# Four chained transformer layers on one core: layer 3 scales its probabilities ahead of the value product, with a second query buffer and a revised planner

## The chip, the cores and the metric

The kernel runs on one core of one Trainium2 chip. The metric is the device time of one execution in microseconds (us). Three runs of the kernel before gave 2625.58, 2627.42 and 2633.65 us, a median of 2627.42.

## What is computed

There are 64 batches of 128 tokens with 128 features. A context of 77 tokens per batch is shared by the first three layers. Every layer has 16 heads. Layers 0, 1 and 2 are cross-attention layers with heads of 8 features; layer 3 is self-attention with heads of 64 features, in segments of 64 tokens. Cut to layer 3, the reference is:

```
q, k, v = split(rms_norm(x) @ to_qkv_w)        # 16 heads x 64 features
q, k = rope(q), rope(k)
kf = [k_extra x 16, persistent keys x 16, k]   # k_extra: one row per batch, 16 times
vf = [v_extra x 16, persistent values x 16, v]
scores = q . kf * 64**-0.5, masked: causal and same segment, or extra/persistent
probs = softmax(scores)
x = x + (probs . vf) @ to_out_w
x = x + (silu(g) * a) @ ff_w2 + ff_b2          # a, g from rms_norm(x) @ ff_w1
```

The 16 extra keys are equal, so the kernel holds one of them and gives its exponential the weight NM = 16. Per segment there are then KE = 64 + 1 + 16 = 81 keys.

## The kernel before, in words

**Order of the work.** Nothing is issued while the kernel function runs. Each engine call is recorded by a planner (`Plan`, L56). It holds a model of the cost of each operation (`matmul` for TensorE, `other` for the rest, from L137 on), gives each a start time, and at the end issues all calls in the order of those times (`issue`). So the order on every engine's queue, SyncE's DMA queue among them, comes out of the model, and the chip then follows that fixed order, with semaphores for the true dependencies. The layers are written as generators ("threads") in two chains: chain 0 holds layers 0 to 2, chain 1 holds layer 3. The main loop proceeds with the thread whose next operands are ready first; `ahead` is the lead in TensorE work of chain 0 over chain 1, in units of WORK = 71 us, less LEAD = 1.4, and moves the choice towards the chain that is behind. `SWITCH` prices a change of TensorE's tile shape.

**Fills.** Where the planner sees TensorE idle for over 0.4 us, `keep_busy` puts in matmuls whose result nobody reads (`first16` by `ident16`, bf16, 512 or 128 columns), until 0.1 us short of the awaited start. They are in TensorE's stream for good, and their line in the profile is that of the matmul that they precede.

**Tiling.** Layers 0 to 2 go by groups of G = 4 batches (16 groups), and layer 3 by batch within a group. Layers 0 to 2 share `attend` (scores at L675/L684, maximum L696, subtraction L697, exponential L700, transposes of the probabilities by `turned` L635/L636, values L719, division by the sums after the product L739/L741).

**Layer 3, one batch.** `layer3_ahead` computes `rms_scaled` once per group (POOL multiplies four 128x128 blocks at L555) and then, batch by batch, `layer3_projections`: q and k with rotation (`rope`: matmuls L1078, DVE shuffle L1080, POOL L1081 and L1086, DVE L1085) and v (L1108, copied by ACT at L1110/L1111 into `vext` and `vs`; a DMA brings the second segment over). `vext` has 65 columns per head: 64 values and a one, so the value product also gives the sum of the probabilities; the memory row holds 16 times its values and a 16. `layer3_middle` runs `layer3_scores` in two halves of eight heads: a penalty product (L1129: bf16 identity of 128x128 by a mask of 4x81 columns, two per half), then 16 products of 64x64 tiles (L1135), the maximum (DVE L1143) and the subtraction (DVE L1144); one exponential over all 16 heads follows (ACT L1150). `layer3_values` transposes the probabilities (L635/L636) and, in two halves, multiplies them with `vext` (L1171, 81x64 tiles, probabilities stationary, two column tiles), takes the reciprocal of the sum column (L1179), multiplies (DVE L1180) into `o`, transposes `o` with eight 128x128 transposes (L1196, ACT copies L1197) into `oT`, and multiplies with the output weights (L1202, L1204). `layer3_feed_forward` runs once per group. There is one buffer each of `q3`, `o3` and `oT3`. `layer3_ahead` starts the projections of batch i when the scores of i-1 are recorded and the values of i-2.

PSUM has two double banks `sc` (scores, layer 3's values, hidden layers) and four single banks `mm`.

Of the kernel before, what the change touches and what calls it, by code (L numbers as in the profile page):

```python
# [20 lines left out]
P = 128  # L21
# [30 lines left out]

WORK, LEAD = 71.0, 1.4


class Plan:  # L56
# [16 lines left out]
    def __init__(self):  # L73
        self.records = []
        self.lines = {}
        self.past = {}
        self.free = {}
        self.tags = {}
        self.pe, self.shape, self.work = 0.7, (128, 128), 0.0
        self.window, self.use, self.clock = 0.0, 0.0, 1.0  # L80
        self.idle = None
        self.lost, self.switched, self.fills = 0.0, 0.0, 0
        self.block = 0.0, 0.0
# [32 lines left out]

    def after(self, x, write, engine):

        t = 0.0
        p0, p1, f0, f1 = self.reach(x)  # L120
        for q0, q1, g0, g1, own, other, by, wrote in self.past.get(x.name, ()):
            if (write or wrote) and q0 < p1 and p0 < q1 and g0 < f1 and f0 < g1:
                t = max(t, own if by == engine else other + self.SEM)
        return t

    def access(self, x, write, own, other, engine):
# [12 lines left out]
    def matmul(self, dst, w, x, passes, call, line):  # L139
# [15 lines left out]
        else:  # L155
            cost = max(cost * 1.02, 0.05 if half else 0.109)
        cost *= passes
        self.work += cost
        start = max(
            self.pe, self.after(dst, True, "PE"), self.after(w, False, "PE"),  # L160
            self.after(x, False, "PE"),
        )
        if self.idle is not None and start - self.pe > self.FILL:
            self.keep_busy(start - 0.1, shape, line)
        self.run(start, shape, cost, call, line)
        end = self.pe + (0.2 if self.clock == 1.0 else 0.3)
# [3 lines left out]

    def run(self, start, shape, cost, call, line):
        while start - self.window > self.WINDOW:
            share = self.use / self.WINDOW
            self.clock = 0.5 if share < self.SLOW else 1.0 if share > self.FAST else self.clock
            self.use = 0.0
            self.window += self.WINDOW
        switch = self.switch(shape)
        cost /= self.clock
        self.use += switch + cost
        self.lost += cost * (1 - self.clock)  # L180
        self.switched += switch
        self.records.append((start, len(self.records), call, line))
        self.pe = start + switch + cost
        self.shape = shape
# [40 lines left out]
    def other(self, engine, op, args, kw, call, line):  # L225
# [24 lines left out]
        name = engine  # L250
        t = max(0.7, self.pe - self.BEHIND)
        for x in aps:
            t = max(t, self.after(x, any(x is o for o in outs), engine))
        takes = max(cost - hidden, 0.02)
# [76 lines left out]
def four_layers(ctx: ExitStack, tc: tile.TileContext, a: dict, out: bass.AP):  # L331
# [105 lines left out]
    def load_x(g):  # L437
# [6 lines left out]
        {  # L444
            "h": (1, FF * G * P), "o3": (1, 8 * P), "oT3": (1, 8 * P), "q3": (1, 8 * P),
            "vs": (1, 8 * P), "ro": (3, 4 * P),
# [99 lines left out]
    def rms_scaled(x, name):  # L546
# [7 lines left out]
        for b in range(G):  # L554
            pool.tensor_scalar(y[:, b, :], x[:, b, :], r[:, b : b + 1], None, ALU.mult)  # L555
        drop(mv, ms, r)
# [356 lines left out]
    def memory_tokens():  # L913


        mT = const.tile([P, B], F32, tag="mT", name="mT")
        parts = [(att, "s3", H * KE)] * 2 + [(p3, tag, 8 * P) for tag in ("q3", "o3", "oT3")]
        i = 0
# [10 lines left out]
        kmem = const.tile([P, 8, B], F32, tag="kmem", name="kmem")  # L929
        vmem = const.tile([B, H, DH3 + 1], F32, tag="vmem", name="vmem")  # L930
        yield "wait", lambda: 0 in ys or done[0] > 0
# [26 lines left out]
        acte.copy(kmem, pm)  # L958
        dve.memset(vmem[:, :, DH3], float(NM))
        for c in range(2):  # L960
            yield F, tokT, "mm"
            pm = bank([B, 512], f"mem_p4{c}")
            w = wqkv[:, (16 + 4 * c) * P : (20 + 4 * c) * P]
            matmul(pm, tokT, w, start=True, stop=True)

            acte.activation(
                vmem[:, 8 * c : 8 * c + 8, 0:DH3],
                pm.rearrange("p (h d) -> p h d", d=DH3),
                AF.Copy,
                scale=float(NM),  # L970
            )
# [4 lines left out]
    kext = [in_p3.tile([P, 8, 2, KE], F32, tag=f"kext{i}", name=f"kext{i}") for i in range(2)]  # L976
    vext = [in_p3.tile([KE, 2, H, DH3 + 1], F32, tag=f"vext{i}", name=f"vext{i}") for i in range(2)]
    for i in range(2):
        dve.memset(vext[i][:, :, :, DH3], 1.0)
        for s in range(2):  # L980
            sp.dma_start(kext[i][:, :, s, SEG + 1 : KE], a["L3_pmK"])
            sp.dma_start(vext[i][SEG + 1 : KE, s, :, 0:DH3], a["L3_pmV"])
# [135 lines left out]
    def layer3_scores(i, qT):  # L1118
# [4 lines left out]
        for half in range(2):  # L1123
            yield F, qT, kx, "sc"
            pb = two_banks(f"{n}_ps{half}")
            ps = pb[:, :, : 4 * KE].rearrange("p c (j k) -> p c j k", k=KE)
            for c in range(2):
                pen = pen316.unsqueeze(1).to_broadcast([P, 4, KE])
                matmul(ps[:, c], ident16, pen, start=True, stop=False)  # L1129
            for j in range(4):  # L1130
# [11 lines left out]
            m = mx[:, 8 * half : 8 * half + 8].rearrange("p (c j) -> p c j", c=2)  # L1142
            dve.tensor_reduce(m, ps, AX.X, ALU.max)  # L1143
            dve.tensor_tensor(  # L1144
                sc[:, 8 * half : 8 * half + 8, :].rearrange("p (c j) k -> p c j k", c=2),
                ps,
                m.unsqueeze(3).to_broadcast([P, 2, 4, KE]),
                ALU.subtract,
            )
        acte.activation(sc, sc, AF.Exp, scale=DH3**-0.5)  # L1150
        drop(mx, qT)
        return sc

    def layer3_values(i, sc, x):
        n = f"a3_{i}"
        vx = vext[i % 2]
        o = p3.tile([P, 2, 4, 2, DH3], F32, tag="o3", name=f"{n}_o")
        sT = att.tile([KE, H, P], F32, tag="sT3", name=f"{n}_sT")
        for j in range(0, H, 4):
            yield from turned(sT, j, sc.rearrange("p h k -> p (h k)"), KE, n)  # L1160
        drop(sc)
        turned3[0] = i + 1
        for half in range(2):
            yield (128, 64), sT, "sc"
            pb = two_banks(f"{n}_pa{half}")
            pa = pb[:, :, : 4 * (DH3 + 1)].rearrange("p c (j d) -> p c j d", j=4)
            for c in range(2):
                for j in range(4):
                    slot = 4 * (2 * half + c) + j
                    for s in range(2):  # L1170
                        matmul(  # L1171
                            pa[SEG * s : SEG * s + SEG, c, j, :],
                            sT[:, slot, SEG * s : SEG * s + SEG],
                            vx[:, s, head(slot), :],
                            start=True,
                            stop=True,
                        )
            rs = small.tile([P, 2, 4], F32, tag="rsl3", name=f"{n}_rs{half}")
            dve.reciprocal(rs, pa[:, :, :, DH3])  # L1179
            dve.tensor_tensor(  # L1180
                o[:, half].rearrange("p j e d -> p e j d"),
                pa[:, :, :, 0:DH3],
                rs.unsqueeze(3).to_broadcast([P, 2, 4, DH3]),
                ALU.mult,
            )
            drop(rs)
        drop(sT)
        valued3[0] = i + 1
        of = o.rearrange("p a j e d -> p (a j e d)")
        oT = p3.tile([P, 8, P], F32, tag="oT3", name=f"{n}_oT")  # L1190
        for half in range(2):
            yield F, o, "mm"
            pt = bank([P, 4, P], f"{n}_po{half}")
            for j in range(4):
                c = 4 * half + j
                transpose(pt[:, j, :], of[:, c * P : (c + 1) * P])  # L1196
            acte.copy(oT[:, 4 * half : 4 * half + 4, :], pt)  # L1197
        drop(o)
        yield F, oT, "mm"
# [6 lines left out]
    def layer3_feed_forward(g, y):  # L1206
        x = xs[g]
        xT = yield from transposed(y, f"f3_{g}_xT", fnorm, tag="x3")
        drop(y)
        xT = xT.rearrange("p b t -> p (b t)")  # L1210
        u01 = p3.tile([P, 2, G * P], F32, tag="oT3", name=f"f3_{g}_u01")
        u2 = p3.tile([P, 2, G * P], F32, tag="o3", name=f"f3_{g}_u2")
        uT = [u01[:, 0, :], u01[:, 1, :], u2[:, 0, :]]
        for c, (o0, n) in enumerate(FF3):
# [42 lines left out]
    idle = Tiles(  # L1257
        xT=(act, "xT"), kT=(p3, "vs"), v=(p3, "o3"), qT=(p3, "q3"), o=(act, "y3"),
        kb=(p3, "ro"), s=(att, "s3"), sT=(att, "sT3"), w=(act, "x3"),
    )  # L1260

    def early_layer0():
        for g in range(1, 1 + early):
            yield "wait", lambda: fed[0] >= g and begun[0] >= g and plan.free["cT"]
            cT = load_ctx(g)
# [6 lines left out]
    def layers_0_to_2():  # L1272
        yield begun0_at
        o, ready = yield from begun0
        yield "also", layer0_feed_forward(0, o, ready)
        yield "also", early_layer0()
        for g in range(NG):
# [23 lines left out]
    def layer3_ahead():  # L1301
        for i in range(B):
            g, b = divmod(i, G)
            if b == 0:
# [3 lines left out]
                drop(y)  # L1308
            yield "wait", lambda: scored3[0] >= i and valued3[0] >= i - 1
            qs[i] = yield from layer3_projections(i, xT[:, b, :])  # L1310
# [147 lines left out]
```

## Time and profile before

| what | value |
|---|---|
| median of the three runs | 2627.42 us |
| the profiled execution | 2622.82 us |
| its span, first to last instruction | 2621.0 us |
| instructions | 64439 |
| mean granted TensorE clock | 0.983 |
| TensorE (PE) busy | 2473.2 us, 94% |
| VectorE (DVE) busy | 1908.2 us, 73% |
| ScalarE (ACT) busy | 1372.1 us, 52% |
| GpSimd (POOL) busy | 1368.8 us, 52% |
| mean busy share of the DMA engines | about 20% |

"Busy" is the time in which at least one instruction of the engine runs. A float32 matmul stands as two records, and a record runs from its entry to its last result, which is longer than the time after which the next may enter; the rates below are therefore taken from runs of many. A group's row gives line, engine, operation, what is written from what, shapes and count; then busy us and mean ns of one; then the idle time of the engine just before the group, and what ended it. The chain of work is followed back from the last instruction, and its shares tell on which engine and line the time was spent.

### The profile page before, as it was taken

The numbers are of one execution on the slowest core, as the hardware profiler recorded it, in microseconds if no ns is written. First come the engines' busy times: TensorE is split into PE (matmuls) and PEld (weight loads), VectorE is DVE, ScalarE is ACT, GpSimd is POOL, SyncE is SP. The second block draws the span as 40 slices with busy tenths as digits, with TensorE's granted clock in tenths as the row PEclk, the third lists the DMA queues.
The fourth block names the chain that finished last, engine by engine and source line by source line (L and its number), as shares of the span: only waits on it lengthen the run. The fifth ranks groups of instructions, "written<-read, shape, count | busy, mean of one in ns | idle before, by whom it ended". The sixth has DMA issues, their size and how long they took to land.

```text
span 2621.0 us, 64439 instructions
## 1 busy us (share of the span) xinstructions
PE 2473.2 (94%) x26568; PEld 1810.8 (69%) x26568; DVE 1908.2 (73%) x3973; ACT 1372.1 (52%) x2361; POOL 1368.8 (52%) x1421
## 2 busy tenths in 40 slices
PE   7999999999899999999999999999999999999998
PEld 3566776767667776767767777677776667767776
DVE  4656787777877778676876868688775977777664
ACT  2455454556464555546555555545555555554543
POOL 1234646454754655455564645656454654637563
PEclk8999999999999999999999999999999999999999
DMA  5311221212122121211212121211212112121010
GB/s 115 107 26 38 49 41 30 62 27 46 28 47 45 26 66 18 51 34 35 52 20 70 23 49 31 49 39 25 70 17 49 40 32 52 22 58 17 12 19 14
DMA packets 376479, 108.21 MB, mean 41 GB/s; under 512 B 328739, under 2 KB 364920, under 8 KB 376056
## 3 DMA queue, kind: packets, MB, share of 16 engines
q1 hardware_dynamic: 376184, 104.08, 19.4%
q8 instruction: 209, 3.42, 0.5%
q14 instruction: 86, 0.70, 0.1%
HBM read 74.97 MB, written 4.19 MB: 30 GB/s over the span
## 4 chain that ended last, share of the span: by engine, by line
PE 57%; DVE 26%; POOL 6%; issue 5%; ACT 2%; DMA 2%; SPq 1%; DVEq 0%; POOLq 0%; ACTq 0%
PE mm L635 9%; PE mm L1078 5%; PE sc L684 5%; PE mm L567 5%; DVE mx L696 4%; PE sc L825 3%; PE sc L1171 3%; PE mm L719 3%; DVE s L697 3%; DVE s L1003 3%; PE mm L1108 3%; PE mm L1202 3%; DVE s L1001 2%; PE sc L1135 2%; DVE ro L1080 2%
## 5 line engine op out<-in xcount | busy, mean ns | idle before, releaser
L636 ACT COPY sT<-mm 116x512 f32<-116x512 f32 (+2 forms) x832 | 443.3, 585 | 185.6 <-PE mm L635 177.6
L1081 POOL TENSOR_TENSOR ro<-ro,w_c_sin 128x512 f32<-128x512 f32 x256 | 327.6, 1280 | 388.5 <-DVE ro L1080 386.6
L635 PE MATMUL mm<-w_c_ident,s 128*116 128x128 f32 (+2 forms) x3328 | 459.7, 281 | 56.7 <-DVE q L1085 11.2
L700 ACT ACTIVATE s<-s 128x616 f32<-128x616 f32 x384 | 275.4, 717 | 444.2 <-DVE s L697 442.9
L635 PEld LDWEIGHTS mm<-w_c_ident,s 128*116 128x116 f32 (+2 forms) x3328 | 376.2, 145 | 147.9 <-issue 45.5
L520 POOL TENSOR_TENSOR rstd<-rstd,mhalf 128x4 f32<-128x4 f32 x96 | 102.6, 1068 | 401.2 <-DVE rstd L519 384.3
L652 POOL TENSOR_TENSOR kb<-kT,qmask 128x308 f32<-128x308 f32 x184 | 131.8, 726 | 339.7 <-PE sc L684 176.7
L1078 PE MATMUL mm<-x,w_L_to_qkv_w 128*128 128x128 f32 x2048 | 266.2, 279 | 4.1 <-ACT sT L636 2.6
L684 PE MATMUL sc<-kb,qT 32*128 32x308 f32 x1472 | 257.8, 460 | 10.4 <-DVE s L1144 5.5
L696 DVE TENSOR_REDUCE mx<-sc 128x8 f32<-128x616 f32 x256 | 202.8, 792 | 86.4 <-PE sc L684 85.8
L1078 PEld LDWEIGHTS mm<-x,w_L_to_qkv_w 128*128 128x128 f32 x2048 | 243.8, 192 | 24.9 <-issue 12.7
L697 DVE TENSOR_TENSOR s<-sc,mx 128x616 f32<-128x616 f32 x256 | 204.6, 799 | 9.1
L1080 DVE STREAM_SHUFFLE ro<-mm 128x512 f32<-128x512 f32 x256 | 188.3, 735 | 0.6
L719 PE MATMUL mm<-sT,vf 116*32 116x128 f32 (+1 forms) x4608 | 170.7, 278 | 7.0 <-ACT sT L636 4.4
L1086 POOL TENSOR_TENSOR q<-q,ro 128x512 f32<-128x512 f32 x128 | 164.3, 1284 | 10.0
L719 PEld LDWEIGHTS mm<-sT,vf 116*32 116x32 f32 (+1 forms) x4608 | 116.2, 110 | 76.6 <-issue 29.8
L1086 POOL TENSOR_TENSOR kext<-kext,ro 128x512 f32<-128x512 f32 x128 | 155.2, 1212 | 10.0
L1143 DVE TENSOR_REDUCE mx<-sc 128x8 f32<-128x648 f32 x128 | 105.8, 827 | 67.2 <-PE sc L1135 66.3
L1150 ACT ACTIVATE s<-s 128x1296 f32<-128x1296 f32 x64 | 82.2, 1284 | 137.8 <-DVE s L1144 137.6
L684 PEld LDWEIGHTS sc<-kb,qT 32*128 32x128 f32 x1472 | 108.1, 187 | 64.8 <-issue 39.0
L1171 PEld LDWEIGHTS sc<-vext,sT 81*64 81x64 f32 x4096 | 129.2, 139 | 31.0 <-issue 15.4
L1171 PE MATMUL sc<-vext,sT 81*64 81x65 f32 x4096 | 141.6, 226 | 3.8 <-DVE s L697 3.1
(228 smaller groups left out, 4849.1 us busy)
## 6 DMA issues: line engine op xcount, KB each, us to landing
s<-in_fside SPq DMA_DIRECT2D x64, 616.0 KB
vext<-vs SPq DMA_DIRECT2D x64, 256.0 KB
fm<-in_fmask SPq DMA_DIRECT2D x64, 154.0 KB
vf<-v SPq DMA_DIRECT2D x138, 38.5 KB
cT<-in_ctxT SPq DMA_DIRECT2D x32, 154.0 KB
xT<-in_xT SPq DMA_DIRECT2D x16, 256.0 KB
xs<-in_x SPq DMA_DIRECT2D x16, 256.0 KB
out<-y SPq DMA_DIRECT2D x16, 256.0 KB
```

Source lines behind the costliest of these rows:

```text
L635: transpose(pt[:, i, :], s[:, columns(keys, j + i)])
L636: acte.copy(dst[:keys, j : j + 4, :], pt)
L684: matmul(ps[:, c], qT[r, b * P : (b + 1) * P], kb[r], start=pen is None, stop=True,)
L696: dve.tensor_reduce(m, ps, AX.X, ALU.max)
L697: dve.tensor_tensor(d, ps, m.unsqueeze(3).to_broadcast([P, 2, QD, S2]), ALU.subtract)
L700: acte.activation(s[:, h0 : h0 + 8], s[:, h0 : h0 + 8], AF.Exp, scale=scale)
L719: matmul(pa[VC * c : VC * c + VC, x // 2, :], va[:r, x, b, c], sT[:r, j, :], start=x != 1, stop=x != 0,)
L1078: matmul(pq[:, j, :], w, xT, start=True, stop=True)
L1080: dve.stream_shuffle(ro, pq, swap)
L1081: pool.tensor_tensor(ro, ro, sinT.unsqueeze(1).to_broadcast([P, 4, P]), ALU.mult)
L1086: pool.tensor_tensor(d, d, ro, ALU.add)
L1171: matmul(pa[SEG * s : SEG * s + SEG, c, j, :], sT[:, slot, SEG * s : SEG * s + SEG], vx[:, s, head(slot), :], start=True, stop=True,)
```

## The change

- Layer 3 normalises before the value product. The exponential is taken per half; POOL multiplies the memory key's probability by 16, DVE sums, DVE takes the reciprocal, POOL multiplies. `vext` loses its column of ones (65 to 64 columns), and the memory values their factor 16.
- The value product is turned around: `vext` is stationary and the probabilities stream, so that its result is already transposed; the tile `o`, its reciprocal and multiplication, and the eight transposes per batch go. It writes one `mm` bank per half in place of a double bank.
- The penalty product is done in four 64x64 tiles per half.
- `q3` has two buffers, `o3` goes; projections may start one batch earlier. The feed-forward's third block moves from `o3` to `q3`.
- `rms_scaled` multiplies on ACT, not POOL.
- The early layer-0 groups start before the first group's end.
- The planner charges each further semaphore wait of an instruction with 0.05 us (PE, DVE) or 0.017 us, and LEAD is 1.8.

```diff
-WORK, LEAD = 71.0, 1.4
+WORK, LEAD = 71.0, 1.8
...
+    def waits(self, engine, ends):
+        new = [by for by, end in ends.items() if end > self.known.get((engine, by), 0.0)]
+        self.known.update(((engine, by), ends[by]) for by in new)
+        return max(0, len(new) - 1) * (0.05 if engine in ("PE", "DVE") else 0.017)
...
-        self.run(start, shape, cost, call, line)
+        self.run(start, shape, cost, call, line, self.waits("PE", ends))
...
+        cost += self.waits(engine, ends)
...
-            "h": (1, FF * G * P), "o3": (1, 8 * P), "oT3": (1, 8 * P), "q3": (1, 8 * P),
+            "h": (1, FF * G * P), "oT3": (1, 8 * P), "q3": (2, 8 * P),
...
-            pool.tensor_scalar(y[:, b, :], x[:, b, :], r[:, b : b + 1], None, ALU.mult)
+            acte.activation(y[:, b, :], x[:, b, :], AF.Copy, scale=r[:, b : b + 1])
...
-    vext = [in_p3.tile([KE, 2, H, DH3 + 1], F32, tag=f"vext{i}", name=f"vext{i}") for i in range(2)]
+    vext = [in_p3.tile([KE, 2, H, DH3], F32, tag=f"vext{i}", name=f"vext{i}") for i in range(2)]
...
             for c in range(2):
-                pen = pen316.unsqueeze(1).to_broadcast([P, 4, KE])
-                matmul(ps[:, c], ident16, pen, start=True, stop=False)
+                r = slice(SEG * c, SEG * c + SEG)
+                pen = pen316[r].unsqueeze(1).to_broadcast([SEG, 4, KE])
+                for s in range(2):
+                    q = slice(SEG * s, SEG * s + SEG)
+                    matmul(ps[q, c], ident16[r, r], pen, start=True, stop=False)
...
-        acte.activation(sc, sc, AF.Exp, scale=DH3**-0.5)
+            acte.activation(ex, ex, AF.Exp, scale=DH3**-0.5)
+            pool.tensor_scalar(ex[:, :, SEG], ex[:, :, SEG], float(NM), None, ALU.mult)
+            total = small.tile([P, 8], F32, tag="rsl3", name=f"{n}_t{half}")
+            dve.tensor_reduce(total, ex, AX.X, ALU.add)
+            dve.reciprocal(total, total)
+            pool.tensor_tensor(
+                ex, ex, total.unsqueeze(2).to_broadcast([P, 8, KE]), ALU.mult
+            )
...
-            yield (128, 64), sT, "sc"
-            pb = two_banks(f"{n}_pa{half}")
+            yield (128, 64), sT, "mm"
+            pa = bank([P, 4, P], f"{n}_pa{half}")
-            for c in range(2):
-                for j in range(4):
+            for j in range(4):
+                for c in range(2):
                     slot = 4 * (2 * half + c) + j
                     for s in range(2):
                         matmul(
-                            pa[SEG * s : SEG * s + SEG, c, j, :],
+                            pa[DH3 * c : DH3 * c + DH3, j, SEG * s : SEG * s + SEG],
+                            vx[:, s, head(slot), :],
                             sT[:, slot, SEG * s : SEG * s + SEG],
-                            vx[:, s, head(slot), :],
...
-            rs = small.tile([P, 2, 4], F32, tag="rsl3", name=f"{n}_rs{half}")
-            dve.reciprocal(rs, pa[:, :, :, DH3])
-            dve.tensor_tensor(
...
+            acte.copy(oT[:, 4 * half : 4 * half + 4, :], pa)
...
-                transpose(pt[:, j, :], of[:, c * P : (c + 1) * P])
-            acte.copy(oT[:, 4 * half : 4 * half + 4, :], pt)
...
+        yield "wait", free("q3")
-        u2 = p3.tile([P, 2, G * P], F32, tag="o3", name=f"f3_{g}_u2")
+        u2 = p3.tile([P, G * P], F32, tag="q3", name=f"f3_{g}_u2")
...
-            yield "wait", lambda: fed[0] >= g and begun[0] >= g and plan.free["cT"]
+            yield "wait", lambda: fed[0] >= g - 1 and begun[0] >= g - 1 and plan.free["cT"]
...
-            yield "wait", lambda: scored3[0] >= i and valued3[0] >= i - 1
+            yield "wait", lambda: scored3[0] >= i - 1 and valued3[0] >= i - 1 and plan.free["q3"]
```

More of the change, by code (lines that the diff above doesn't have):

```diff
@@ L80, in __init__ @@
         self.window, self.use, self.clock = 0.0, 0.0, 1.0
+        self.known = {}
         self.idle = None
@@ L115, in reach, with after @@
         return p, p + parts, f, f + 1 + sum(abs(s) * (c - 1) for s, c in free)
-    def after(self, x, write, engine):
+    def after(self, x, write, engine, ends=None):
         t = 0.0
@@ L123, in after @@
                 t = max(t, own if by == engine else other + self.SEM)
-        return t
+                if ends is not None and by != engine:
+                    ends[by] = max(ends.get(by, 0.0), other)
+        return t
+    def waits(self, engine, ends):
+        new = [by for by, end in ends.items() if end > self.known.get((engine, by), 0.0)]
+        self.known.update(((engine, by), ends[by]) for by in new)
+        return max(0, len(new) - 1) * (0.05 if engine in ("PE", "DVE") else 0.017)
     def access(self, x, write, own, other, engine):
@@ L158, in matmul @@
         self.work += cost
+        ends = {}
         start = max(
-            self.pe, self.after(dst, True, "PE"), self.after(w, False, "PE"),
-            self.after(x, False, "PE"),
+            self.pe, self.after(dst, True, "PE", ends), self.after(w, False, "PE", ends),
+            self.after(x, False, "PE", ends),
         )
@@ L169, in matmul, with run @@
         self.access(x, False, self.pe, end, "PE")
-    def run(self, start, shape, cost, call, line):
+    def run(self, start, shape, cost, call, line, extra=0.0):
         while start - self.window > self.WINDOW:
@@ L176, in run @@
             self.window += self.WINDOW
-        switch = self.switch(shape)
+        switch = self.switch(shape) + extra
         cost /= self.clock
@@ L251, in other @@
         t = max(0.7, self.pe - self.BEHIND)
+        ends = {}
         for x in aps:
-            t = max(t, self.after(x, any(x is o for o in outs), engine))
+            t = max(t, self.after(x, any(x is o for o in outs), engine, ends))
+        cost += self.waits(engine, ends)
         takes = max(cost - hidden, 0.02)
@@ L916, in memory_tokens @@
         mT = const.tile([P, B], F32, tag="mT", name="mT")
-        parts = [(att, "s3", H * KE)] * 2 + [(p3, tag, 8 * P) for tag in ("q3", "o3", "oT3")]
+        parts = [(att, "s3", H * KE)] * 2 + [(p3, tag, 8 * P) for tag in ("q3", "vs", "oT3")]
         i = 0
@@ L929, in memory_tokens @@
         kmem = const.tile([P, 8, B], F32, tag="kmem", name="kmem")
-        vmem = const.tile([B, H, DH3 + 1], F32, tag="vmem", name="vmem")
+        vmem = const.tile([B, H, DH3], F32, tag="vmem", name="vmem")
         yield "wait", lambda: 0 in ys or done[0] > 0
@@ L958, in memory_tokens @@
         acte.copy(kmem, pm)
-        dve.memset(vmem[:, :, DH3], float(NM))
         for c in range(2):
@@ L964, in memory_tokens @@
             matmul(pm, tokT, w, start=True, stop=True)
[L966 to L970, printed above, removed]
+            acte.copy(
+                vmem[:, 8 * c : 8 * c + 8, :], pm.rearrange("p (h d) -> p h d", d=DH3)
             )
@@ L976, in four_layers @@
     kext = [in_p3.tile([P, 8, 2, KE], F32, tag=f"kext{i}", name=f"kext{i}") for i in range(2)]
-    vext = [in_p3.tile([KE, 2, H, DH3 + 1], F32, tag=f"vext{i}", name=f"vext{i}") for i in range(2)]
+    vext = [in_p3.tile([KE, 2, H, DH3], F32, tag=f"vext{i}", name=f"vext{i}") for i in range(2)]
     for i in range(2):
-        dve.memset(vext[i][:, :, :, DH3], 1.0)
         for s in range(2):
@@ L1123, in layer3_scores @@
         for half in range(2):
-            yield F, qT, kx, "sc"
+            yield (64, 64), qT, kx, "sc"
             pb = two_banks(f"{n}_ps{half}")
@@ L1143, in layer3_scores @@
             dve.tensor_reduce(m, ps, AX.X, ALU.max)
+            ex = sc[:, 8 * half : 8 * half + 8, :]
             dve.tensor_tensor(
-                sc[:, 8 * half : 8 * half + 8, :].rearrange("p (c j) k -> p c j k", c=2),
+                ex.rearrange("p (c j) k -> p c j k", c=2),
                 ps,
@@ L1149, in layer3_scores @@
             )
-        acte.activation(sc, sc, AF.Exp, scale=DH3**-0.5)
+            acte.activation(ex, ex, AF.Exp, scale=DH3**-0.5)
[6 more added lines that the diff above has]
+            )
+            drop(total)
         drop(mx, qT)
@@ L1156, in layer3_values @@
         vx = vext[i % 2]
-        o = p3.tile([P, 2, 4, 2, DH3], F32, tag="o3", name=f"{n}_o")
         sT = att.tile([KE, H, P], F32, tag="sT3", name=f"{n}_sT")
@@ L1162, in layer3_values @@
         turned3[0] = i + 1
+        oT = p3.tile([P, 8, P], F32, tag="oT3", name=f"{n}_oT")
         for half in range(2):
-            yield (128, 64), sT, "sc"
-            pb = two_banks(f"{n}_pa{half}")
-            pa = pb[:, :, : 4 * (DH3 + 1)].rearrange("p c (j d) -> p c j d", j=4)
-            for c in range(2):
-                for j in range(4):
+            yield (128, 64), sT, "mm"
+            pa = bank([P, 4, P], f"{n}_pa{half}")
+            for j in range(4):
+                for c in range(2):
                     slot = 4 * (2 * half + c) + j
@@ L1177, in layer3_values @@
                         )
-            rs = small.tile([P, 2, 4], F32, tag="rsl3", name=f"{n}_rs{half}")
-            dve.reciprocal(rs, pa[:, :, :, DH3])
[L1180 to L1186, printed above, removed]
+            acte.copy(oT[:, 4 * half : 4 * half + 4, :], pa)
         drop(sT)
         valued3[0] = i + 1
[L1189 to L1198, printed above, removed]
         yield F, oT, "mm"
@@ L1210, in layer3_feed_forward @@
         xT = xT.rearrange("p b t -> p (b t)")
+        yield "wait", free("q3")
         u01 = p3.tile([P, 2, G * P], F32, tag="oT3", name=f"f3_{g}_u01")
-        u2 = p3.tile([P, 2, G * P], F32, tag="o3", name=f"f3_{g}_u2")
-        uT = [u01[:, 0, :], u01[:, 1, :], u2[:, 0, :]]
+        u2 = p3.tile([P, G * P], F32, tag="q3", name=f"f3_{g}_u2")
+        uT = [u01[:, 0, :], u01[:, 1, :], u2]
         for c, (o0, n) in enumerate(FF3):
@@ L1257, in four_layers @@
     idle = Tiles(
-        xT=(act, "xT"), kT=(p3, "vs"), v=(p3, "o3"), qT=(p3, "q3"), o=(act, "y3"),
+        xT=(act, "xT"), kT=(p3, "vs"), v=(p3, "oT3"), qT=(p3, "q3"), o=(act, "y3"),
         kb=(p3, "ro"), s=(att, "s3"), sT=(att, "sT3"), w=(act, "x3"),
@@ L1273, in layers_0_to_2 @@
         yield begun0_at
+        yield "also", early_layer0()
         o, ready = yield from begun0
         yield "also", layer0_feed_forward(0, o, ready)
-        yield "also", early_layer0()
         for g in range(NG):
```

## The prediction

> **What bounds the kernel now.** I read the page first: the busy shares, the chain that ended last, then the rows of groups with shapes kept apart, then the time-ordered chain inside one steady stretch.
>
> ```profile
> span 2621.0 us, 64439 instructions
> PE 2473.2 (94%) x26568; PEld 1810.8 (69%) x26568; DVE 1908.2 (73%) x3973; ACT 1372.1 (52%) x2361; POOL 1368.8 (52%) x1421
> PE   7999999999899999999999999999999999999998
> PE 57%; DVE 26%; POOL 6%; issue 5%; ACT 2%; DMA 2%; SPq 1%; DVEq 0%; POOLq 0%; ACTq 0%
> ```
>
> TensorE is busy from the third slice to the end and carries 57% of the chain, VectorE 26%. 2621.0 - 2473.2 = 148 us are without any matmul: by stretches of the trace, 26 us in the first 262, 106 up to 2424, 15 in the last 197. So a matmul taken out pays only if nothing else then holds TensorE up, and VectorE at 73% is the next.
>
> ```profile
> L1171 PE MATMUL sc<-vext,sT 81*64 81x65 f32 x4096 | 141.6, 226 | 3.8 <-DVE s L697 3.1 <-DVE s L1144 0.4
> L1196 PE MATMUL mm<-w_c_ident,o 128*128 128x128 f32 x512 | 74.4, 278 | 3.1 <-DVE o L1180 2.1 <-ACT oT L1197 0.3
> L1129 PE MATMUL sc<-pen,ident 128*128 128x324 bf16 x256 | 56.9, 303 | 4.9 <-DVE s L697 1.8 <-ACT h L827 1.1 <-DVE o L1226 0.6
> L684 PE MATMUL mm<-first,ident 32*128 32x512 bf16 x109 | 26.9, 390 | 0.0
> L1180 DVE TENSOR_TENSOR o<-sc,rsl 128x512 f32<-128x512 f32 x128 | 88.5, 691 | 4.4
> L1081 POOL TENSOR_TENSOR ro<-ro,w_c_sin 128x512 f32<-128x512 f32 x256 | 327.6, 1280 | 388.5 <-DVE ro L1080 386.6 <-ACT s L700 1.7
> L697 DVE TENSOR_TENSOR s<-sc,mx 128x616 f32<-128x616 f32 x256 | 204.6, 799 | 9.1
> L697 DVE TENSOR_TENSOR s<-s,mx 128x616 f32<-128x616 f32 x128 | 120.8, 944 | 4.3
> ```
>
> These are the rows that the change touches or resembles. A matmul's mean holds its latency, so I take rates from runs in the chain in order of time:
>
> ```profile
> 1210.16 0.28 PE sc L1129 x2
> 1210.44 0.77 PE sc L1135 x32
> ...
> 1227.71 1.08 PE sc L1171 x32
> ...
> 1235.72 0.88 PE mm L1196 x8
> ```
>
> **TensorE, what goes.** 512 transposes (L1196) at 0.88/8 = 0.11 us: -56 us (their row's 74.4 holds the tails of 128 sets too, which the next matmul covers). The penalty: two of 0.14 us per half become four in four different 64x64 tiles. If those run side by side, one 0.14 us is left: 128 halves x 0.14 = -17 us. L1135 speaks for it: 32 records of 81 columns in 0.77 us, 24 ns each, against 236 for one. If they ran one after another it would be 0.56 us per half, +35. I take -17. The built programs' TensorE streams have 1139 changes of tile shape after, 1237 before; between the end of the last penalty's 0.14 us (1210.27) and the first L1135 (1210.37) the timeline leaves 0.1 us, so 98 x 0.1 = -10. One column of 65 less: -2. Sum **-85 us**.
>
> **TensorE, what comes.** The built streams hold 608 fills before and 1122 after: 505 to 963 of 512 columns, 103 to 159 of 128. By the row above, 26.9/109 = 0.247 us each (0.14 for the short, L635's 17 took 2.3): 458 x 0.247 + 56 x 0.14 = **+121 us**. By stretches of the stream (first tenth of the real matmuls, middle, last 7.5%) it is 351/160/97 fills before, 311/538/273 after. A fill runs whether or not the wait it covers exists. So TensorE's stream grows by 121 - 85 = +36 us although real work leaves it: the planner sees TensorE waiting longer for others. How much of this falls into idle time is the whole question. The same program with the new charge for waits set to nothing has 910 fills; so 212 of them (50 us) answer to waits that the planner of before did not see, though the chip had them: TensorE's 148 idle us are those. The other 302 (71 us) answer to real waits of the new order. Value taken: the 50 us fall into idle time, so 2621 + 36 - 50 = **2607 us** span. Bounds: none falls there, 2657; or, with the better costs, a third of the 98 us of idle then left goes as well, 2573.
>
> **VectorE.** Out: 128 x 691 (L1180) = -88 us; 128 reciprocals move, 0.2 us each, at nothing. In: 128 sums of 648 columns; the maximum of 616 from SBUF takes 795 ns, so 836 ns: +107. Net +19, 1927 us (74%). It lies beside TensorE in the middle, but all of it is ahead of the values now.
>
> **POOL.** In: 128 products of 648 columns at 1280/512 = 2.5 ns: 1.62 us, +207. 128 multiplications of 8 columns: between the 16-column copy (L1102, 260 ns) and the 128-column L555 (606 ns); taken 0.3, +38. Out: L555, -75. Net +170, 1539 us (59%). Behind each new product on POOL's queue stand rope's L1081/L1086, at 1.28 us each, and layer norms; a rope late by 2 us is hidden while projections run one batch ahead, and costs the 2 us where layer 3 is alone. [...]
>
> **ACT.** The exponential in halves: L700 (616 columns) 717, so 744 ns x 128 - 82 = +13; 128 scalings of 128 columns, L728 at 256 takes 368 ns, taken 0.32: +41. 1426 us (54%), hidden by TensorE. The copies of `oT` stay.
>
> **Latency of a half of layer 3's softmax.** Added: 0.3 + 0.84 + 0.2 + 1.62 = 3.0 us between exponential and transposes; removed behind the values: 0.2 + 0.69 + the transposes' 0.44 and their wait. The second query buffer and scores one batch ahead cover it, with 2621/64 = 41 us per batch. In the last stretch, where layer 3 is alone, the cover is gone; the 176 more fills there (about 40 us) show that, and LEAD 1.8 lengthens this stretch.
>
> **DMA, start.** `vext` rows become contiguous (256-byte pieces become 4 KB); DMA is 2% of the chain, so nothing. On SyncE's queue the early group's x and context move ahead of the second kext load; fills fall from 351 to 311 there, about -10, already in the sum.
>
> **The value product.** Passes now come to one column tile four in a row (two products of two passes), before two and two. No row shows four. L719 has two in a row over four tiles and still keeps them side by side. With side by side kept, 0. If the queue blocked behind a busy tile, eight passes would take 6 slots in place of 4: 64 records in 2.02 us (L1171 in the same chain) are 32 ns each, half more is 4096 x 16 = +65 us. I take 0, by L719.
>
> **The rivals.** (a) As taken: 2607, plus the 1.8 us between span and profiled time, 2609; the median of the runs shown is 4.6 above the profiled one, so 2613. Chance 0.38; own range 2600 to 2630. (b) The new cost model is nearer the chip, waits are filled and ordered better: 2573 span, 2580. For it: three quarters of the idle lies in the middle in small waits. Against: real work in the stream is only 85 us less. Chance 0.22. (c) The other side: fills are too long. The planner charges the 8-column multiplication 1.26 us, where rows say 0.3; TensorE then works through fills for probabilities that are already there, and none of the 121 us falls into idle: 2657 + 6 = 2663. It decides as soon as less than 36 us are covered. Chance 0.25. (d) The column tiles block: 2613 + 65 = 2678; chance 0.09. (e) POOL's longer queue holds up rope in the middle too, 1 us per batch: 2613 + 64 = 2677; 0.06.
>
> **How the numbers follow.** Predicted 2613. The range leaves out the outer parts of (b) and of (c) to (e): 2562 to 2670. About 0.3% (8 us) can be told from no change: faster is below 2619.5: most of (a), 0.27, with (b), 0.49; within: 0.14; slower 0.37.
>
> **What would show it.** PE: L1196 gone; the penalty about 0.14 us per half; the value product at 64 records in 2.0 us (in (d) 3.0); 1122 fills at about 260 us; idle without matmuls about 100 us (in (c) still near 150, in (b) 70). VectorE near 1927, POOL near 1540, ACT near 1426 us. POOL's new product at 1.6 us, waiting on VectorE; its 8-column one at 0.3. Wrong would be: POOL or VectorE above 40% of the chain, or a last stretch longer by more than 40 us.

## The result and the profile after

The changed kernel takes 2664.72 us (median of 4 runs, 2663.23 to 2668.99), the kernel before 2626.85 (4 runs). The ratio is 1.0145, 95% interval 1.0126 to 1.0163: 1.45% slower, where 0.5% faster was forecast. The time lies inside the range, and on rival (c)'s 2663.

The page of the changed kernel: its span, the busy shares, TensorE's granted clock in 40 slices, and the chain by engine. The last line is the same clock in the kernel before.

```profile
span 2667.2 us, 65345 instructions
...
PE 2523.3 (95%) x26826; PEld 1815.2 (68%) x26826; DVE 1911.6 (72%) x3970; ACT 1420.6 (53%) x2553; POOL 1490.2 (56%) x1549
...
PEclk8999999999989999989999999999999999999999
...
PE 59%; DVE 25%; POOL 5%; issue 4%; ACT 4%; DMA 1%; SPq 1%; DVEq 0%; POOLq 0%; ACTq 0%
```

```profile
PEclk8999999999999999999999999999999999999999
```

TensorE became busier by 50 us although the transposes are gone, and the time without any matmul is 2667.2 - 2523.3 = 144 us, as before (148). The shares of VectorE and GpSimd in the chain did not grow. So the time is in TensorE's own stream. Its rows with shapes kept apart (the largest groups of fills, then the new value product, the new penalty, and the new operations on the other engines; last, from the kernel before, the fills that stood before layer 3's score products and before the old penalty):

```profile
L1138 PE MATMUL mm<-first,ident 64*64 64x512 bf16 x227 | 58.0, 410 | 0.1
L647 PE MATMUL mm<-first,ident 128*128 128x512 bf16 x178 | 47.1, 413 | 0.1
L687 PE MATMUL mm<-first,ident 32*128 32x512 bf16 x139 | 39.6, 441 | 0.0
L520 PE MATMUL mm<-first,ident 128*128 128x512 bf16 x154 | 35.2, 379 | 0.0
L696 PE MATMUL mm<-first,ident 32*128 32x512 bf16 x100 | 28.7, 430 | 0.5 <-DVE o L753 0.5
...
L1189 PE MATMUL mm<-sT,vext 81*64 81x64 f32 x4096 | 140.9, 225 | 1.6 <-ACT sT L648 0.7 <-DVE rs L751 0.4 <-DVE o L753 0.3
L1138 PE MATMUL sc<-pen,ident 64*64 64x324 bf16 x512 | 47.0, 324 | 5.2 <-DVE s L709 2.6 <-DVE q L1227 1.3 <-DVE s L1007 0.5
L1166 POOL TENSOR_TENSOR s<-s,rsl 128x648 f32<-128x648 f32 x128 | 164.0, 1281 | 219.2 <-DVE rsl L1165 196.8 <-DVE st L539 11.9 <-PE mm L647 2.8
L1162 POOL TENSOR_SCALAR s<-s 128x8 f32<-128x8 f32 x128 | 33.6, 262 | 183.0 <-ACT s L1160 175.6
L567 ACT ACTIVATE y<-xs,rstd 128x128 f32<-128x128 f32 x128 | 40.8, 391 | 50.0 <-POOL rstd L532 49.9
```

```profile
L1135 PE MATMUL mm<-first,ident 64*64 64x512 bf16 x36 | 8.1, 377 | 0.0
L1129 PE MATMUL mm<-first,ident 128*128 128x512 bf16 x13 | 3.6, 381 | 0.0
```

The value product in the chain, 64 records before (L1171) and after (L1189):

```profile
1262.65 2.02 PE sc L1171 x64
```

```profile
1024.42 2.06 PE mm L1189 x64
```

Two things are to be seen. By the rows of fills a 512-column fill occupies 0.23 to 0.29 us, and a tile of 64 or 32 rows (58.0/227, 39.6/139) is no cheaper than one of 128 (35.2/154, 47.1/178). And over half of the fills now lie on tiles of 64 or 32 rows: 591 of 1122 in the trace, against 247 of 608 before, with most of the growth on 64 rows (316 for 38).

For every block of fills I took three times from each trace: its length (first fill's start to the next real matmul's start), when the last producer that this matmul waits for ended, and how much of the block came after that, called late below. The late part hangs on which producer is taken to end a wait, so e1 tests it. "Waits" is idle time plus the part of the fills that is not late. Half speed is the time at a granted clock of 0.5, with up to 3 us of it behind the last instruction.

| kernel | median us | ratio [95%] | fills | fill us | late us | idle us | waits us | half speed us |
|---|---|---|---|---|---|---|---|---|
| before | 2626.85 | 1 | 608 | 131 | 26 | 148 | 253 | 91 |
| changed | 2664.72 | 1.0145 [1.0126, 1.0163] | 1122 | 241 | 83 | 144 | 302 | 158 |
| e1_trim | 2614.85 | 0.9955 [0.9938, 0.9971] | 733 | 174 | 11 | 178 | 340 | 122 |
| e2_planner_only | 2686.81 | 1.0232 [1.0216, 1.0247] | 890 | 185 | 35 | 147 | 296 | 108 |
| e3_body_only | 2798.28 | 1.0647 [1.0611, 1.0683] | 1557 | 336 | 96 | 170 | 410 | 186 |
| e4_prices | 2636.21 | 1.0044 [1.0024, 1.0063] | 806 | 154 | 34 | 173 | 293 | 163 |
| e5_before_lead | 2679.52 | 1.0193 [1.0176, 1.0210] | 815 | 175 | 35 | 160 | 301 | 100 |
| e6_after_nocharge | 2666.51 | 1.0144 [1.0129, 1.0159] | 910 | 208 | 76 | 171 | 304 | 182 |
| e7_fill_price | 2616.16 | 0.9951 [0.9936, 0.9966] | 863 | 196 | 23 | 163 | 335 | 116 |
| e8_full_rows | 2642.07 | 1.0054 [1.0037, 1.0070] | 1122 | 240 | 84 | 149 | 305 | 53 |
| e9_before_fills | 2613.35 | 0.9940 [0.9927, 0.9952] | 501 | 131 | 9 | 159 | 280 | 85 |
| e10_after_fills | 2609.30 | 0.9926 [0.9913, 0.9938] | 863 | 202 | 27 | 164 | 340 | 70 |
| e11_after_all | 2612.60 | 0.9937 [0.9924, 0.9949] | 619 | 158 | 14 | 191 | 336 | 127 |
| e12_all_lead2 | 2604.52 | 0.9907 [0.9893, 0.9921] | 680 | 184 | 16 | 190 | 359 | 92 |
| e13_scale_pool | 2657.32 | 1.0123 [1.0108, 1.0138] | 863 | 206 | 28 | 185 | 363 | 143 |
| e14_product_dve | 2655.85 | 1.0124 [1.0103, 1.0145] | 863 | 207 | 28 | 196 | 375 | 81 |

Ratios are to runs of the kernel before on the same chip, with medians of 2625.76 to 2628.19 us.

The theory formed from the trace: fills put in for waits that were shorter than the planner took them to be. Late fills rose by 57 us. Its rivals: layer 3's longer softmax chain really holds TensorE, or the new planner's charge and LEAD make a worse order.

### The profile page after: what moved, and what is told of

Same layout as the page of the kernel before. It is cut to its first block, busy times and chain, and to the rows that moved or that the text cites. A ratio compares the mean times of both kernels' runs of the same rounds, so it can differ in the third digit from the quotient of the medians.

```text
span 2667.2 us, 65345 instructions
## 1 busy us (share of the span) xinstructions
PE 2523.3 (95%) x26826; PEld 1815.2 (68%) x26826; DVE 1911.6 (72%) x3970; ACT 1420.6 (53%) x2553; POOL 1490.2 (56%) x1549
## 4 chain that ended last, share of the span: by engine, by line
PE 59%; DVE 25%; POOL 5%; issue 4%; ACT 4%; DMA 1%; SPq 1%; DVEq 0%; POOLq 0%; ACTq 0%
PE mm L647 10%; PE mm L1084 6%; PE sc L696 5%; PE mm L579 4%; DVE mx L708 4%; PE mm L1189 4%; PE mm L1202 3%; PE mm L731 3%; PE sc L837 3%; DVE s L709 3%; PE mm L1114 3%; DVE s L1009 2%; DVE s L1007 2%; PE mm L520 2%; PE mm L1138 2%
## 5 line engine op out<-in xcount | busy, mean ns | idle before, releaser
L1087 POOL TENSOR_TENSOR ro<-ro,w_c_sin 128x512 f32<-128x512 f32 x256 | 328.0, 1281 | 146.9 <-DVE ro L1086 146.4
L1166 POOL TENSOR_TENSOR s<-s,rsl 128x648 f32<-128x648 f32 x128 | 164.0, 1281 | 219.2 <-DVE rsl L1165 196.8
L1007 DVE TENSOR_TENSOR s<-sc,s 128x616 f32<-128x616 f32 x128 | 101.2, 791 | 72.4 <-PE sc L696 72.0
L1189 PEld LDWEIGHTS mm<-sT,vext 81*64 81x64 f32 x4096 | 130.2, 138 | 27.5 <-issue 9.0
```

The source lines that it names most:

```text
L1087: pool.tensor_tensor(ro, ro, sinT.unsqueeze(1).to_broadcast([P, 4, P]), ALU.mult)
L1189: matmul(pa[DH3 * c : DH3 * c + DH3, j, SEG * s : SEG * s + SEG], vx[:, s, head(slot), :], sT[:, slot, SEG * s : SEG * s + SEG], start=Tru ...
```

## The experiments

**e1_trim: the late fills out, all else in place.** LATE lists 389 of the 1122 fills by their numbers. Nothing that the output needs is left out, since nobody reads a fill's result.

```diff
+LATE = [(0, 5),
+(10, 18),
...
+            if number in self.fill_records:
+                at += 1
+                if any(p <= at < q for p, q in LATE):
+                    continue
```

> The changed kernel with 389 of its 1122 fills left out: those that in its trace began after the operand that the next real matmul waits for was there (83 us of fill time in all stood so, against 26 us in the kernel before). The order of all else is the same. Theory A (fills that outlast the wait they were put in for cost the time): 40 to 83 us less than the changed kernel's 2665, so 2582 to 2625. Theory B (TensorE is held by the later links of layer 3's longer softmax chain, and the fills only stand where it would be idle): within 10 us of 2665. Theory C (the fills also keep the clock up, so that their loss is paid back in half-speed windows): 2665 or more, with a granted clock below 0.95.

Measured: 2614.85, 50 us less than the changed kernel and 0.45% less than the one before.

```profile
span 2613.5 us, 64568 instructions
...
PE 2435.9 (93%) x26437; PEld 1772.1 (68%) x26437; DVE 1910.0 (73%) x3970; ACT 1421.6 (54%) x2553; POOL 1490.7 (57%) x1549
```

TensorE is busy 87 us less, the time falls by 50, and 34 us turn into idle. This is theory A. Theory C falls, since half-speed time went down with the fills (158 to 122 us); a part of the 50 is therefore the clock's, an estimated 8 us at the rate that e8 shows below (23 us of time for 105 at half speed). The late fills turned a gain into a loss.

**e2 and e3: planner and kernel body taken apart.** e2 is the kernel before with the changed `Plan` and LEAD; e3 the changed kernel with the old ones.

> The kernel before with the new planner alone (the charge for further waits, LEAD 1.8); layer 3 and the rest as before. It holds 890 fills for 608. Theory A (fills): 282 more fills are 67 us, of which part falls into idle time: 2640 to 2670. Theory B (layer 3's new order costs the time): within 10 us of 2627.

> The changed kernel with the old planner (no charge for waits, LEAD 1.4). It holds 1557 fills. Theory A: 435 more fills than the changed kernel are 100 us, partly in real waits: 2690 to 2760. Theory B (layer 3's order costs, the planner does not): 2655 to 2680. If the new planner were the culprit and the body a gain: below 2627.

```diff
-WORK, LEAD = 71.0, 1.4      # e2: into the kernel before; e3 is the reverse, in the changed one
+WORK, LEAD = 71.0, 1.8
...
+        cost += self.waits(engine, ends)
```

e2 took 2686.8 and e3 2798.3, both above everything expected: the new planner costs the old body 60 us, and the old planner costs the new body 134. Given the new planner, the new body is 22 us better than the old. Only 9 us of e2's loss are late fills; its waits rose by 43 us, so most of this is order.

**e5 and e6: LEAD and the charge taken apart.**

```diff
-WORK, LEAD = 71.0, 1.4      # e5, in the kernel before
+WORK, LEAD = 71.0, 1.8
...
-        return max(0, len(new) - 1) * (0.05 if engine in ("PE", "DVE") else 0.017)   # e6, in the changed one
+        return 0.0
```

> The kernel before with LEAD 1.8 for 1.4, nothing else. It holds 815 fills for 608. The new planner as a whole cost the kernel before 61 us. If LEAD is what costs: 2670 to 2700. If the charge for waits is: within 15 us of 2626.

> The changed kernel without the charge for further waits, LEAD 1.8 kept. It holds 910 fills for 1122. My prediction took the 212 fills between them to stand in idle time, at no cost. Theory A (these fills are paid for): 2610 to 2640. If the charge makes the order better, as the prediction had it: 2670 to 2700.

e5 took 2679.5: LEAD alone makes nearly all of e2's loss. e6 took 2666.5 against 2664.7: with these fills, the charge for waits is worth nothing either way, and neither expectation of e6 was met. Its row in the table says why: with the charge, fills are 33 us more and idle is 27 us less. Those fills did fall into idle time, as predicted, but of an order that without them idles 171 us and not 148. And e3 against e6 (2798 and 2667, LEAD 1.4 and 1.8, both without the charge) shows that the new body needs the LEAD that hurts the old one.

**e4_prices: the two POOL operations at their measured price.**

```diff
-                cost = {2: 1.26, 3: 0.6, 4: 0.8}[len(aps)]
+                cost = 0.25 if n <= 8 and len(aps) == 2 else {2: 1.26, 3: 0.6, 4: 0.8}[len(aps)]
+            elif n == 8 * KE:
+                cost = 1.28
```

> The changed kernel with two prices of the planner set to what the trace of the changed kernel shows: the 8-column multiplication 0.25 us for 1.26, the 648-column product 1.28 us for 1.605. It holds 806 fills for 1122. Theory A (the two overpriced POOL operations make the planner hold TensorE back with fills for probabilities that are ready): 2600 to 2635. Theory B (the real chain is what holds TensorE): 2655 to 2670.

2636.2, 29 us less, a microsecond above the span of theory A. Late fills fall from 83 to 34 us. The planner had charged 1.26 us for 0.26 and 1.61 for 1.28, 1.3 us too much in each of 128 halves of the softmax. The new prices also move the work: in the traces, two thirds of the places in TensorE's stream of real matmuls hold another matmul than in the changed kernel. So the 29 us are those of fills and order together, and of both prices.

**e7_fill_price: what a fill costs on a small tile.** The planner takes a fill on fewer than 128 rows at half price, so it puts in twice as many as fit.

```diff
-            cost = n * 0.00041667 * (1.0 if rows == P else 0.5)
+            cost = n * 0.00041667
```

> The changed kernel with one factor of keep_busy mended: the planner counts a 512-column fill on a tile of less than 128 rows as 0.107 us, while the rows of the trace give 0.25 to 0.29 us for such a fill on 32 or 64 rows. With the same price for all shapes there are 863 fills for 1122, and the real matmuls stand in the same order. Theory A (fills outlast their waits because of that price): about half of the 50 us that leaving out the late fills gave, 2632 to 2650. If the lateness comes from elsewhere: within 8 us of 2665.

2616.2, 49 us less; I had expected about 25. The real matmuls stand in the same order, 259 fills fewer. As in e1, half-speed time fell too (158 to 116 us), an estimated 9 us of the 49 at e8's rate. Two of the rows above, in this kernel's trace:

```profile
L1138 PE MATMUL mm<-first,ident 64*64 64x512 bf16 x110 | 29.4, 411 | 0.1
L687 PE MATMUL mm<-first,ident 32*128 32x512 bf16 x65 | 17.4, 407 | 0.0
```

227 became 110 and 139 became 65. By these rows one still occupies 0.27 us. This one factor, already in the kernel before, undoes more than the whole loss. It weighed less there: the same mend takes 107 fills out of that kernel (e9), 259 out of this one. The changed penalty product stands on a 64-row tile at the head of every score half, and 250 fills (L1138) stand before it.

**e8_full_rows: fills and the clock.** In the changed kernel's trace, TensorE from 749 us on: stretch, its length, then busy time and count of TensorE, weight loads, VectorE, ACT and POOL, then granted clock.

```profile
749.00:754.00 5.00, 5.00 (x24) 2.10 (x22) 1.99 (x3) 2.45 (x4) 4.21 (x5) 0.95 0.26 56
754.00:774.00 20.00, 20.00 (x94) 10.29 (x93) 4.49 (x6) 2.04 (x3) 0.26 (x1) 0.50 0.00 0
```

The order of time shows what the first 5 us were, and the chain the whole run of fills that they belong to:

```profile
748.20 6.11 PE L687 MATMUL mm<-first,ident 32*128 32x512 bf16 x26
```

```profile
747.61 15.04 PE mm L687 x49
```

For 15 us TensorE did nothing but fills on 32 rows, without a pause. Yet its clock was halved 5.9 us after the first of them, at 753.5, and stayed so for 20.5 us, past their end. TensorE was busy for all of the 5.00 us of the first row, so its busy share alone did not hold the clock. The half-speed stretches of this trace last 3.41 us or multiples of it (20.5 us here), but for the last, of 0.84 us.

```diff
-        w = w[:rows, :cols]
+        w = w if rows == 32 else w[:rows, :cols]
+        depth = P if rows == 32 else rows
...
-                some = x[:rows].unsqueeze(1).to_broadcast([rows, n // P, P])
+                some = x[:depth].unsqueeze(1).to_broadcast([depth, n // P, P])
```

> The changed kernel with the fills that precede matmuls on 32-row tiles issued over all 128 rows, same number and place. In the traces TensorE's clock was halved for 20.5 us from 753 us on after 24 fills on 32 rows that had kept it 100% busy. Theory A (32-row fills do not count as activity for the clock): half-speed time falls from 158 us to 120 or less, and the total by 10 to 20 us. Against it: changes of tile shape around such fills, 0.1 us each. If rows do not matter: within 6 us of 2665 and about 158 us at half speed.

2642.1, 23 us less, slightly more than theory A's 20; half-speed time 53 us for 158. The same place with the fills on all rows:

```profile
745.00:750.00 5.00, 5.00 (x24) 2.21 (x23) 1.03 (x2) 2.55 (x6) 4.84 (x5) 1.00 0.25 55
750.00:770.00 20.00, 20.00 (x173) 12.31 (x172) 7.13 (x11) 8.11 (x13) 2.69 (x4) 1.00 0.12 31
```

173 matmuls in 20 us for 94, at full clock. So in this place the clock fell to 0.50 with the fills on 32 rows and stayed at 1.00 with them on 128.

No run changes the rows of the 64-row fills, but the changed kernel's trace shows them both ways. From 839.1 us on, 34 fills on 64 rows run at full clock and keep it; from 763.8 us on, behind the 32-row fills above, 64-row work runs at half speed and does not bring the clock back:

```profile
839.10:846.20 7.10, 7.10 (x34) 3.51 (x34) 6.89 (x15) 1.99 (x5) 2.87 (x4) 1.00 0.01 3
846.20:852.00 5.80, 5.80 (x125) 4.78 (x124) 4.68 (x7) 3.11 (x6) 0.29 (x1) 1.00 0.01 3
763.80:768.40 4.60, 4.60 (x14) 1.83 (x15) 1.60 (x2) 0.72 (x1) 0.00 (x0) 0.50 0.00 0
```

The traces of the kernel before and of the changed one show it in more places. I cut them into slots of 3.41 us in step with the changes of the clock and took the slots that matmuls of one height, real ones or fills, occupy to 95% or more. After a slot of 32-row matmuls the next slot was at half speed in 13 of 13 cases (7 came from full clock). Slots of 64 rows kept a full clock in 12 of 12 cases and restored a halved one in 0 of 4. Slots of more than 64 rows kept it in 470 of 470 and restored it in 22 of 23.

**e9 to e12: the mends in both kernels.** e9 and e10 join the edits of e7 and e8, in the kernel before and in the changed one; e11 adds e4's prices; e12 sets LEAD to 2.0 on top.

```diff
-            cost = n * 0.00041667 * (1.0 if rows == P else 0.5)   # e9 to e12
+            cost = n * 0.00041667
...
-        w = w[:rows, :cols]
+        w = w if rows == 32 else w[:rows, :cols]
...
-WORK, LEAD = 71.0, 1.8      # e12
+WORK, LEAD = 71.0, 2.0
```

> The kernel before with both mends of the fills (one price for all tile shapes; fills before 32-row matmuls issued on all 128 rows). 501 fills for 608, same order of the real matmuls. Its trace shows only 26 us of late fills, against 83 in the changed kernel, and 91 us at half speed against 158. Theory A (the fault was in the planner of before too, but the change is what made it heavy): 2605 to 2620. If the fault weighs the same in both: 2560 to 2580.

> The changed kernel with both mends of the fills. The price alone gave 2616, all rows alone 2642, from 2665. Late fills and half-speed windows are two costs; where they add up: 2590 to 2605. If fewer fills leave nothing for the second mend: 2610 to 2618.

> The changed kernel with both mends of the fills and the two measured prices for POOL. 619 fills. If what is left then is real work, of which the change removed 85 us, and the waits are as before: 2560 to 2590. If the longer softmax chain of layer 3 takes the gain back: 2595 or more.

> As the one with all mends, with LEAD 2.0 for 1.8. 680 fills, fewer in the last tenth (30 us of columns for 36). LEAD was worth 52 us the wrong way in the kernel before and over 100 us the right way in the changed one, so the order is touchy: 2565 to 2600, either side of the one with 1.8.

e9 took 2613.4, as theory A has it; e10 2609.3, just above its expected 2590 to 2605, since the two mends overlap; e11 2612.6, against 2560 to 2590 if only real work were left; e12 2604.5, just above its range. The POOL prices, 29 us in e4, bring nothing once the fills are mended (e11 against e10), which fits a gain that came by way of the fills; the order differs too, as in e4. With the fills mended in both, the change is worth 4 us (ratios 0.9926 and 0.9940 to the same runs, with intervals that overlap), although it takes about 80 us of real work from TensorE (the sum is below). Between e9 and e10 waits rose by 60 us and late fills by 18, and ate it. e11's expectation names what that means: the gain is taken back by real waiting, though not yet by which. e12 beats both kernels: 0.93% below the one before. The kernel before was not tried with mended fills and another LEAD.

**e13 and e14: which waits.** Counted as in the table, with the fills that cover a wait, 65 us of TensorE's waits end with ACT before and 113 after. Both kernels start from e10 and change the engine of one operation at its place in the order. That the normalising product is cheaper on POOL was my estimate from the rows of before: 207 us there, with 6% of the chain, against 128 x 0.84 = 107 us on VectorE (799 ns for 616 columns at L697), with 26%.

```diff
-            acte.activation(y[:, b, :], x[:, b, :], AF.Copy, scale=r[:, b : b + 1])   # e13
+            args = y[:, b, :], x[:, b, :]
+            call = partial(nc.gpsimd.tensor_scalar, *args, r[:, b : b + 1], None, ALU.mult)
...
-            pool.tensor_tensor(                                                     # e14
-                ex, ex, total.unsqueeze(2).to_broadcast([P, 8, KE]), ALU.mult
-            )
+            args = ex, ex, total.unsqueeze(2).to_broadcast([P, 8, KE]), ALU.mult
+            call = partial(nc.vector.tensor_tensor, *args)
...
```

> The changed kernel with both mends of the fills, and in it the 128 scalings of the norm issued on POOL again, at the same places of the otherwise unchanged order. In the trace of the changed kernel TensorE waits 23.7 us for ACT's scalings, against 5.4 us for POOL's before. If the move to ACT made these waits: up to 18 us less than 2609, so 2591 to 2604. If the wait is that of the layer norm before it, whichever engine scales: 2605 to 2625.

> The same base with the 128 normalising products of 648 columns issued on VectorE in place of POOL, at the same places of the order. The prediction held POOL to be the cheaper place: on VectorE they take about 0.85 us each, 109 us more in an order that knows nothing of it. If that holds: 2620 to 2660. If VectorE is slack there and POOL's 1.28 us in the softmax chain hold TensorE up (16.5 us of TensorE's waits end with that product): 2595 to 2609.

e13 took 2657.3, 48 us more than e10, beyond both expectations: in this order ACT is the better place for the scaling. Who waited for whom in e13, and then in e10 (us, times, longest):

```profile
PEld mm L521 <- POOL y L570: 52.6, 79, 3.2
PE mm L521 <- POOL y L570: 32.1, 59, 2.8
```

```profile
PEld mm L521 <- ACT y L568: 16.2, 50, 1.8
...
PE mm L521 <- ACT y L568: 5.1, 6, 1.4
```

e14 took 2655.9, 47 us more, within the 2620 to 2660 expected if POOL is the cheaper place. VectorE's product takes 870 ns, and the chain moves to VectorE; the row in e14, then the chain in e14 and in e10:

```profile
L1169 DVE TENSOR_TENSOR s<-s,rsl 128x648 f32<-128x648 f32 x128 | 111.4, 870 | 0.7
```

```profile
PE 46%; DVE 34%; POOL 9%; issue 6%; ACT 4%; DMA 1%; SPq 1%; DVEq 0%; POOLq 0%; ACTq 0%
```

```profile
PE 52%; DVE 29%; POOL 7%; issue 5%; ACT 4%; DMA 1%; SPq 1%; DVEq 0%; POOLq 0%; ACTq 0%
```

So undoing either placement in this order does not bring the lost 80 us back. Both tests keep an order that was planned for the other engine, so they price a late move, not a plan made for it. What stays open: e10's waits for other engines are more than e9's in nearly every sixth of the span after the first, most in the last (73 us for 41), which fits layer 3's longer chain where it runs alone, but no run isolates it. Nor does a run isolate the second query buffer, the earlier start or the turned value product.

## Why the prediction was wrong, step by step

- **Real work taken from TensorE, -85 us. Right.** With half-speed time counted half (a fill of the run at 747.61 us took 0.216 us before the clock fell and 0.427 us after), the matmuls that are not fills come to 2312 us before and 2231 after, 81 less. The value product runs at 64 records in 2.06 us (2.02 before), so rival (d) falls. The four penalty tiles lie side by side: 128 halves are 47.0 us busy, 0.37 each with the latency of the last, where four in a row would take 0.56 without it.
- **Fills, +121 us.** 131 to 241: +110, of which about 14 are fills at half speed. Near enough.
- **"The 50 us fall into idle time." This is the step that failed.** Idle time was to fall from 148 to about 98; it is 144. These 46 us are most of the 60 by which the span (2667) missed 2607; the other 14 are TensorE's stream, which grew by 50 and not by 36. I took 212 fills by their cause in the planner, and assumed that the remaining 302 covered real waits. In the trace 83 of the 241 us are late, 57 more than before. I saw that small-tile fills cost 0.247 us and used it, but did not set it beside the planner's price of half that, which is in the code. e1 and e7 price the step at 49 to 50 us, of which the clock has about 8 or 9.
- **The clock had no term.** Half-speed time rose from 91 to 158 us, about 33 us of lost work, 14 of it in fills. The trace of before already had a half-speed stretch right after 20 fills on 32 rows, at 214 us.
- **LEAD** I saw only as a longer last stretch. It is the largest single lever of the change: +53 us in the old body (e5), about -130 in the new (e3, e6). Layers 0 to 2 end their last group at 2541.6 us for 2479.0, but what follows is shorter, 126 us for 142.
- **Rival (c)** had the number (2663 for 2664.7) and the right first cause: the 8-column multiplication at 262 ns and a price of 1.26 us; with the product's price that is 29 us (e4). It got 0.25. That its number came out so closely is partly luck: it knew neither the halved price of small-tile fills nor the clock.
- **VectorE, POOL, ACT.** 1911.6, 1490.2 and 1420.6 us busy for 1927, 1539 and 1426. POOL's product took 1.28 us and not 1.62. That POOL is the better place for it than VectorE is what e14 shows, in an order planned for POOL. ACT's scaling took 391 ns for 320.
- **Rival (e)** has no sign: TensorE's waits that end with POOL are 38 us, 41 before, counted with the fills that cover them, and POOL's share of the chain went from 6% to 5%.
- **Two slips of no weight.** A third of 98 off 2607 is 2574, where rival (b) says 2573. And TensorE is above 90% from the second slice of the page, not the third.

The sum from the traces: -81 real work, +110 fills with their share of the clock, about +20 lost to the clock in the real matmuls, -4 idle. That makes +45, and the span grew by 46.

## What to carry to other kernels

Work that is put in to keep an engine busy is real work (in e1, 389 fills less were 87 us less of TensorE's busy time): price it by its own row, per tile shape, and look in the trace how much of it outlasts the wait it covers. Where a planner fixes the order, a removed operation is worth what the new order's waits leave of it: here about 80 us of removed work came to 4. Compare two bodies only once the planner's prices fit both: here the two mends of the fills brought one 55 us and the other about 15.

## What the runs showed of the hardware that was not expected

- A run of 49 fills on 32 rows kept TensorE busy for 15.0 us, and its clock was halved 5.9 us after the first; with these fills on 128 rows (e8) it was 1.00 at the same place, from 745 to 770 us. Over the whole kernel that was 105 us of half-speed time and 23 us of time.
- Matmuls on 64 rows kept a full clock (34 fills, 7.1 us at 1.00; 12 of 12 slots) but did not restore a halved one (0 of 4 slots).
- At full clock a bf16 matmul of 512 columns took 0.22 us on 32, 64 and 128 rows alike, from start to start in the changed kernel's trace: 0.216 us in the fills on 32 rows from 747.61 us to the fall of the clock, 0.217 in the 34 on 64 rows from 839.06 on, and 0.216 in 54 on 128 rows from 60.45 on.
- POOL's product of 648 columns with a factor repeated over 81 columns took 1281 ns, the same as one of 512 columns with a full second operand (1281 ns at L1087). On VectorE it took 870 ns.
- POOL's multiplication of 8 columns took 262 ns.
